# Two fixed places for the experts' weights, filled by indirect gathers on GpSimd that leave out what is already there

## The chip, the core and the metric

The kernel runs on one core of a Trainium2 chip. A core has TensorE (PE, matrix products, with a weight load PEld that runs beside them), VectorE (DVE), ScalarE (ACT), GpSimd (POOL) and SyncE (SP), each with a queue of instructions that it works through in order. DMAs are issued from the queues of SP and POOL here and run on 16 DMA engines. The metric is the device time in microseconds; the kernel before has a median of 381.64 us over 9 runs (379.18 to 387.53 and one of 994.7).

## The reference

2048 rows of 512 features go through a layer norm, and two branches are added to the input: an RWKV attention (three projections, a scan over time, an output projection) and a mixture of 12 experts, of which 8 have weights and 4 pass their input through. Each row goes to its two best experts.

```python
xn = _layernorm(x, axis=-1)
x = x + _L0_attn_ref(xn, ...) + _L0_ffn_ref(xn, ...)

# the expert branch, E = 8 experts with weights, 4 without
probs = softmax(xn @ classifier_w.T)
_, idx = top_k(probs + e_score_correction_bias, 2)
rw = take_along_axis(probs, idx) * 1.5
w_full = sum(one_hot(idx, 12) * rw)
act = silu(xn @ gate_w[e].T) * (xn @ up_w[e].T)      # 512 -> 256, twice
out = sum over e < 8 of w_full[e] * (act @ down_w[e].T)   # 256 -> 512
out = out + xn * sum(w_full[8:])
```

## The kernel before

All products are in float32. The kernel has three parts.

First come the norms (`norm`, L207), the transposes of the normalised rows (`turn_block`, L237), and the router. The normalised rows are also stored to a DRAM tensor `xs` (256 KB per 128 rows), from which the experts' rows are read again. From the router's choice DVE works out a list of tiles: the rows of one expert fill tiles of 128, and the tiles of expert 0 come first, then those of expert 1 and so on. There are 25 tiles in the unrolled code (`TILES`) and a loop for up to 40 (`MAX_TILES`), which this input does not enter. `place_tiles` (L647 to L661) makes `which`, the number of the expert of each tile, and `which_i`, the same as integers; the lines up to L722 make `token_i` (the row that each place of a tile takes), `to_i` (where its result goes) and `wplace` (its weight). These are 128x40 tiles, one column per tile.

Second come the 25 tiles, interleaved with the projections, the scans of the attention and the output projections of the first two blocks of rows. Each tile i is worked in two halves (L847 to L876), five steps of which matter here:

- `gather(i)` (L727): an indirect DMA on POOL reads the tile's 128 rows of 2 KB from `xs` into `xg`, which has two buffers.
- `flip(i)` and `unite(i)` (L769, L777): ACT splits each float into halves of 16 bits (`xp`), a DMA transpose issued from SP turns them (`xq`), and ACT puts them together (`xgT`).
- `fetch(i)` (L738) and `fetch_down(i)` (L751): SP reads the expert's number into a register and issues plain loads of 1 MB (`gw`: gate and up weights) and 0.5 MB (`dw`: down weights), in two alternating buffers each. A load can start when the products of the tile two ahead are done with its buffer.
- `up(i)` (L786) and `activate(i)`: eight instructions of TensorE into `pg`, then tanh on ACT and two products on DVE; `flip_act` and `unite_act` turn the result as above (`ap`, `aq`, `actT`).
- `finish(i)` (L830): four instructions of TensorE into `po`, ACT scales them into `yo`, and an indirect DMA on POOL adds the rows to the output in DRAM. Each such scatter waits for the one before it to land, as both write the output. `add_row` (L963) adds finished rows of the attention to the output, from POOL too.

The order on every queue is written out in the program: `plan` (L988) gives each piece of work a time on a common scale, and the pieces are emitted in order of time. `first_half(i)` emits the products into `pg`, then `fetch(i + 2)` and `gather(i + 3)`; `second_half(i)` emits `flip(i + 2)`, `finish(i - 2)` and `fetch_down(i)`. So the scatter of tile i - 2 stands ahead of the gather of tile i + 4 on POOL, and the loads and the transposes share SP's queue. Before all that, L934 to L953 issue the first two gathers, the loads of the first two tiles, and the first flips; `deferred` (L940) are two DVE adds.

Third, the last blocks of the attention: output rows are read back (`read_out`, L891) when all scatters have landed, the last products are added, and the rows are stored.

Of the kernel before, what the change touches and what calls it, by code (L numbers as in the profile page):

```python
# [59 lines left out]
def layer(ctx: ExitStack, tc: tile.TileContext, x, w_rvk, w_out, decay, first, cls, ebias, gu, down, out):  # L60
# [586 lines left out]
    def place_tiles():  # L647

        later = carve([MAX_TILES, E - 1])
        nc.vector.tensor_tensor(  # L650
            later,
            tiles_f.unsqueeze(2).to_broadcast([P, MAX_TILES, E - 1]),
            ends[:, : E - 1].unsqueeze(1).to_broadcast([P, MAX_TILES, E - 1]),
            ALU.is_ge,
        )
        which = rp.tile([P, MAX_TILES + 1], F32, tag="which", name="which")
        nc.vector.tensor_reduce(which[:, :MAX_TILES], later, AX.X, ALU.add)
        nc.vector.tensor_copy(which[:, MAX_TILES:], ends[:, E - 1 :])
        which_i = const.tile([P, MAX_TILES + 1], I32, tag="which_i", name="which_i")
        nc.vector.tensor_copy(which_i, which)  # L660
        return which_i  # L661


    NK = 2 * NT
# [4 lines left out]
    for m in range(2):  # L669
        ks = slice(m * NT, (m + 1) * NT)  # L670
        nc.vector.tensor_tensor(
            lowhot[:, ks, :],
            lane.unsqueeze(1).to_broadcast([P, NT, P]),
            low[:, m].unsqueeze(2).to_broadcast([P, NT, P]),
            ALU.is_equal,
        )
        nc.vector.tensor_tensor(
            hh,
            tiles128.unsqueeze(1).to_broadcast([P, NT, MAX_TILES]),
            high_b[:, m].unsqueeze(2).to_broadcast([P, NT, MAX_TILES]),  # L680
            ALU.is_equal,
        )
        tok = place.tile([P, NT, NV, MAX_TILES], BF16, tag=f"s{7 + m}", name=f"tok{m}")
        nc.vector.tensor_tensor(  # L684
            tok,
            hh.unsqueeze(2).to_broadcast([P, NT, NV, MAX_TILES]),
            vals[:, m].unsqueeze(3).to_broadcast([P, NT, NV, MAX_TILES]),
            ALU.mult,
        )
        for j in range(NT):  # L690
            k = m * NT + j
            nc.tensor.matmul(pi, lowhot[:, k, :], tok[:, j], start=(k == 0), stop=(k == NK - 1))
        if m == 0:
            which_i = place_tiles()
            fill(5)
    nc.vector.tensor_scalar_mul(wdec, wdec, -1.0)
    cfac = const.tile([P, CC], F32, tag="cfac", name="cfac")
    nc.vector.tensor_add(cfac, first_sb, wdec)
# [36 lines left out]
        )  # L735
        st[i] = {"xg": xg}

    def fetch(i, which=which_i):  # L738

        e = nc.values_load(  # L740
            which[0:1, i : i + 1],
            engines=(SP,),
            min_val=0,
            max_val=E - 1,
            skip_runtime_bounds_check_because="a sum of E - 1 comparisons",
        )
        w = place.tile([P, CC, 2 * INTER], F32, tag=f"s{7 - i % 2}", name=f"gw{i}")
        nc.sync.dma_start(w, gu[bass.ds(e, 1)].rearrange("o p c n -> p (o c) n"))
        st[i].update(w=w, e=e)

    def fetch_down(i):  # L751
# [78 lines left out]
    def finish(i, weight=wplace, to=to_i):  # L830
        po = ps_o.tile([P, C], F32, tag="o", name=f"po{i}")
        for c in range(IC):
            nc.tensor.matmul(  # L833
                po, st[i]["actT"][:, c, :], st[i]["d"][:, c, :], start=(c == 0), stop=(c == IC - 1)
            )
        yo = rows.tile([P, C], F32, tag="rb", name=f"yo{i}")
        nc.scalar.activation(yo, po, AF.Identity, scale=weight[:, i : i + 1])  # L837
        nc.gpsimd.indirect_dma_start(  # L838
            out=out,
            out_offset=bass.IndirectOffsetOnAxis(ap=to[:, i : i + 1], axis=0),  # L840
            in_=yo,
            in_offset=None,
            compute_op=ALU.add,
        )
        del st[i]
# [17 lines left out]
    def second_half(i, n):  # L863

        if i + 1 < n:
            unite(i + 1)
        if i + 2 < n:
            flip(i + 2)
        if i > 1:
            finish(i - 2)  # L870
        if 1 < i < n - 1:
            fetch_down(i)
        if i == n - 2:
            fetch_down(i + 1)
        if i == n - 1:
            finish(i - 1)  # L876
# [156 lines left out]
    with tc.If(count > TILES):  # L1033
        with tc.For_i(TILES, MAX_TILES, 1) as i:
            cols = {}
            for name, a, dt in (
                ("which", which_i, I32), ("token", token_i, I32), ("to", to_i, I32), ("weight", wplace, F32)
            ):
# [4 lines left out]
            fetch_down(0)  # L1043
            turn(0)
            up(0, range(CC))
            activate(0)
# [51 lines left out]
```

## Time and profile before

| | |
|---|---|
| median of 9 runs | 381.64 us |
| profiled execution | 378.44 us, its span 376.7 us |
| TensorE busy | 358.2 us (95% of the span), clock 1.0 |
| DVE busy | 308.7 us (82%) |
| ACT busy | 161.6 us (43%) |
| POOL busy | 91.4 us (24%) |
| bytes moved by DMA | 88.80 MB: 67.85 issued from SP, 20.71 from POOL |
| gw loads | 25 of 1024 KB, 5.6 us from issue to landing (median) |
| dw loads | 25 of 512 KB, 6.9 us |
| gathers of rows (xg) | 25, 5.4 us to landing, 1.15 us of POOL each (mean) |
| scatters to the output | 25, 6.7 us to landing, 1.75 us of POOL each (mean) |
| transposes xq | 25, 6.1 us to landing |

Lines of the profile begin with a time where they come from the timeline: start and length in us, the engine, the line of the kernel (L792), the operation, the tile written and the tiles read, how many instructions were merged (x8), and in brackets how long the engine had been idle and what released it. SPq is SP's queue. In the first view of the page, a row of 40 digits shows the busy share of 40 equal slices of the span, 9 being 90% or more. A line of the waits has the waiting engine and line, whom it waited for, the total in us, how often, and the longest.

### The profile page before, as it was taken

What the parts mean: (1) busy time and instruction counts of PE and PEld (TensorE: products, weight loads), DVE (VectorE), ACT (ScalarE), POOL (GpSimd) and SP (SyncE); (2) the same over time, 40 slices, a digit from 0 to 9 for tenths busy, and PEclk for the clock granted to TensorE, in tenths of its full rate; (3) what the DMA queues carried; (4) which work ended last, traced back from release to release, by engine and by line L of the source; (5) the groups of instructions that cost most, each with busy time, mean ns of one, the idle gap of its engine ahead of it and who ended that gap; (6) DMA issues with size and microseconds to landing.
All of it is one profiled execution on the core that took longest, in us unless ns stands there. A gap on an engine that the chain in (4) does not pass through costs nothing.

```text
span 376.7 us, 3504 instructions
## 1 busy us (share of the span) xinstructions
PE 358.2 (95%) x970; PEld 164.9 (44%) x970; DVE 308.7 (82%) x450; ACT 161.6 (43%) x274; POOL 91.4 (24%) x118
## 2 busy tenths in 40 slices
PE   0999998998999999999999999999999999999995
PEld 0565444443444444444444444444444444444343
DVE  5879899989997997986987769597769786959951
ACT  2777210322554555554556463545254556423000
POOL 5000200220202233322232224143145231122420
PEclk9999999999999999999999999999999999999999
DMA  8997944643667989999799998999999999877494
GB/s 288 404 371 285 335 141 167 224 111 112 181 153 200 258 254 260 215 260 269 217 240 269 266 266 227 262 257 311 259 286 250 302 277 262 157 247 167 87 199 135
DMA packets 63029, 88.80 MB, mean 236 GB/s; under 512 B 42208, under 2 KB 42592, under 8 KB 59232
## 3 DMA queue, kind: packets, MB, share of 16 engines
q1 hardware_dynamic: 55472, 67.85, 61.3%
q0 software_dynamic: 7536, 20.71, 24.1%
q8 instruction: 8, 0.13, 0.1%
q14 instruction: 13, 0.11, 0.1%
HBM read 63.78 MB, written 19.40 MB: 221 GB/s over the span
## 4 chain that ended last, share of the span: by engine, by line
PE 76%; DVE 18%; ACT 3%; issue 2%; DMA 1%; SPq 0%; DVEq 0%; ACTq 0%
PE pg L792 22%; PE po L833 10%; PE pr L408 9%; PE py L325 9%; PE pw L970 7%; PE pz L325 6%; PE px L325 5%; PE pw L918 4%; DVE den L504 3%; DVE tok L684 2%; PE pt L245 1%; DMA x<-in_x_dram 1%; DVE st L212 1%; DVE sums L489 1%; DVE obv L476 1%
## 5 line engine op out<-in xcount | busy, mean ns | idle before, releaser
L792 PE MATMUL pg<-gw,xgT 128*128 128x512 f32 x200 | 90.2, 593 | 1.5 <-ACT xgT L780 1.5
L838 POOL DMA_INDIRECT out_dram<-yo,to_i x25 | 43.8, 1751 | 155.9 <-ACT yo L837 84.6
L408 PE MATMUL pr<-xnT,wrvk 128*128 128x512 f32 x128 | 60.6, 593 | 0.0
L792 PEld LDWEIGHTS pg<-gw,xgT 128*128 128x128 f32 x200 | 37.8, 190 | 49.3 <-issue 45.9
L504 DVE RECIPROCAL den<-den 128x512 f32<-128x512 f32 x16 | 53.5, 3346 | 0.0
L833 PE MATMUL po<-dw,actT 128*128 128x512 f32 x100 | 46.9, 593 | 0.5 <-ACT actT L811 0.5
L800 ACT ACTIVATE th<-pg 128x256 f32<-128x256 f32 x25 | 9.6, 385 | 85.5 <-PE pg L792 85.5
L730 POOL DMA_INDIRECT xg<-xs,token_i x25 | 28.7, 1150 | 61.6 <-ACT xp L772 28.0
L801 DVE SCALAR_TENSOR_TENSOR th<-th,pg 128x256 f32<-128x256 f32 x25 | 10.5, 418 | 32.4 <-ACT th L800 32.2
L408 PEld LDWEIGHTS pr<-xnT,wrvk 128*128 128x128 f32 x128 | 24.1, 190 | 29.2 <-issue 29.2
L325 PE MATMUL px<-xnT,wrvk 128*128 128x512 f32 x64 | 32.3, 604 | 0.0
L780 ACT COPY xgT<-xq 128x1024 uint16<-128x1024 uint16 x25 | 29.0, 1159 | 4.7 <-DMA xq<-xp 4.7
L325 PE MATMUL py<-t,wrvk 128*128 128x512 f32 x64 | 30.7, 594 | 0.0
L918 PE MATMUL pw<-wout_sb,yT 128*128 128x512 f32 (+1 forms) x72 | 28.2, 548 | 2.0 <-DVE xrows L931 1.5
L970 PE MATMUL pw<-wout_sb,yT 128*128 128x512 f32 x64 | 30.1, 592 | 0.0
L833 PEld LDWEIGHTS po<-dw,actT 128*128 128x128 f32 x100 | 18.9, 190 | 24.2 <-issue 22.7
L772 ACT COPY xp<-xg 128x1024 uint16<-128x1024 uint16 x25 | 26.2, 1046 | 5.5 <-DMA xq<-xp 4.3
L837 ACT ACTIVATE yo<-po,wplace 128x512 f32<-128x512 f32 x25 | 17.2, 688 | 22.5 <-PE po L833 22.5
L489 DVE TENSOR_TENSOR_SCAN sums<-obv,state,a 128x512 f32<-128x512 f32 x16 | 20.5, 1282 | 4.0 <-ACT obv L482 3.8
L491 DVE TENSOR_TENSOR_SCAN sums<-obv,state,a 128x512 f32<-128x512 f32 x16 | 20.5, 1284 | 0.6
L918 PEld LDWEIGHTS pw<-wout_sb,yT 128*128 128x128 f32 x72 | 13.5, 190 | 17.0 <-issue 13.4
L476 DVE TENSOR_TENSOR_SCAN obv<-wdec,state,k 128x512 f32<-128x512 f32 x16 | 20.5, 1279 | 0.0
(169 smaller groups left out, 458.1 us busy)
## 6 DMA issues: line engine op xcount, KB each, us to landing
gw<-in_gu_dram SPq DMA_DIRECT2D x25, 1024.0 KB, 5.6
dw<-in_down_dram SPq DMA_DIRECT2D x25, 512.0 KB, 6.9
x<-in_x_dram SPq DMA_DIRECT2D x16, 256.0 KB, 5.4
xs<-x SPq DMA_DIRECT2D x16, 256.0 KB, 7.3
wrvk<-in_w_rvk_dram SPq DMA_DIRECT2D x3, 1024.0 KB
xrow<-xs SPq DMA_DIRECT2D x8, 256.0 KB, 6.1
out_dram<-xrow POOLq DMA_DIRECT2D x8, 256.0 KB, 8.0
xrows<-xs SPq DMA_DIRECT2D x8, 256.0 KB, 5.4
```

The source lines that it names most:

```text
L325: nc.tensor.matmul(ps, a[:, k, c * P : (c + 1) * P], x[:, k], start=(start and k == 0), stop=(k == 1), skip_group_check=True,)
L408: nc.tensor.matmul(ps, wrvk_sb[0][:, k, c * P : (c + 1) * P], xnT[b][:, k, :], start=(k == 0), stop=(k == CC - 1))
L476: nc.vector.tensor_tensor_scan(o2, w.to_broadcast([P, TB]), k, s[:, 0:1], ALU.add, ALU.max)
L504: nc.vector.reciprocal(den, den)
L730: nc.gpsimd.indirect_dma_start(out=xg, out_offset=None, in_=xs, in_offset=bass.IndirectOffsetOnAxis(ap=token[:, i : i + 1], axis=0),)
L772: nc.scalar.copy(xp, st[i]["xg"].bitcast(U16).rearrange("p (c h) -> p h c", h=2))
L780: nc.scalar.copy(xgT.bitcast(U16).rearrange("p c (t h) -> p c t h", h=2), st[i]["xq"].rearrange("p (h c) t -> p c t h", h=2),)
L792: nc.tensor.matmul(pg, st[i]["xgT"][:, c, :], st[i]["w"][:, c, :], start=(c == 0), stop=(c == CC - 1))
L833: nc.tensor.matmul(po, st[i]["actT"][:, c, :], st[i]["d"][:, c, :], start=(c == 0), stop=(c == IC - 1))
L838: nc.gpsimd.indirect_dma_start(out=out, out_offset=bass.IndirectOffsetOnAxis(ap=to[:, i : i + 1], axis=0), in_=yo, in_offset=None, compute ...
L918: nc.tensor.matmul(po[:, hs], yT[b][:, c, j * P : (j + 1) * P], wout_sb[:, c, hs], start=(c == 0), stop=(c == CC - 1),)
L970: nc.tensor.matmul(po, yT[b][:, c, j * P : (j + 1) * P], wout_sb[:, c, :], start=(c == 0), stop=(c == CC - 1))
```

## The change

The places for the weights are no longer taken anew for every tile. Two places for `gw` and two for `dw` are made once, and tile i uses place i % 2 of each. They are filled by indirect gathers issued from POOL: partition p of a place takes row 128 e + p of the weights, seen as 1024 rows of 8 KB (gate and up) or 4 KB (down). The rows' numbers come from `place_rows`, five DVE instructions on 128x40 or 128x38 elements that stand after the last router products are issued: `all_i` holds the number 128 e + p for each tile, and `new_i` the same plus 8192 where the tile two ahead has the same expert. A number beyond the last row is out of bounds, and such rows are not copied. The last tile's down weights go to a place of their own and take `all_i`.

The loads leave SP's queue, and SP reads no expert's number any more. `fetch(i + 2)` stays in `first_half(i)`, so it is now on POOL ahead of `gather(i + 3)`. `fetch_down(i)` moves from the end of `second_half(i)` into `finish(i - 2)`, after its products and ahead of its scatter on POOL. The first two tiles' loads stand on POOL behind the first two gathers. The loop for further tiles uses `all_i`.

```diff
+    def place_rows():
+        row = rp.tile([P, MAX_TILES], F32, tag="row", name="row")
+        nc.vector.tensor_scalar(row, which[:, :MAX_TILES], float(P), tok_p, ALU.mult, ALU.add)
+        all_i = const.tile([P, MAX_TILES], I32, tag="all_i", name="all_i")
+        nc.vector.tensor_copy(all_i, row)
+        same = rp.tile([P, MAX_TILES - 2], F32, tag="same", name="same")
+        nc.vector.tensor_tensor(same, which[:, 2:MAX_TILES], which[:, : MAX_TILES - 2], ALU.is_equal)
+        nc.vector.scalar_tensor_tensor(row[:, 2:], same, FAR, row[:, 2:], ALU.mult, ALU.add)
+        new_i = const.tile([P, MAX_TILES], I32, tag="new_i", name="new_i")
+        nc.vector.tensor_copy(new_i, row)
+        return all_i, new_i
...
         if m == 0:
-            which_i = place_tiles()
+            which, which_i = place_tiles()
             fill(5)
+    all_i, new_i = place_rows()
     nc.vector.tensor_scalar_mul(wdec, wdec, -1.0)
...
-    def fetch(i, which=which_i):
-        e = nc.values_load(
...
-        w = place.tile([P, CC, 2 * INTER], F32, tag=f"s{7 - i % 2}", name=f"gw{i}")
-        nc.sync.dma_start(w, gu[bass.ds(e, 1)].rearrange("o p c n -> p (o c) n"))
...
+    gws = [place.tile([P, CC, 2 * INTER], F32, tag=f"s{7 - n}", name=f"gw{n}") for n in range(2)]
+    dws = [dwp.tile([P, IC, C], F32, tag="dw", name=f"dw{n}") for n in range(2)]
+
+    def load_rows(t, a, rows_i, i):
+        nc.gpsimd.indirect_dma_start(
+            out=t.rearrange("p c n -> p (c n)"),
+            out_offset=None,
+            in_=a.rearrange("e p c n -> (e p) (c n)"),
+            in_offset=bass.IndirectOffsetOnAxis(ap=rows_i[:, i : i + 1], axis=0),
+            bounds_check=E * P - 1,
+            oob_is_err=False,
+        )
+
+    def fetch(i, rows_i=new_i):
+        load_rows(gws[i % 2], gu, rows_i, i)
+        st[i]["w"] = gws[i % 2]
+
+    def fetch_down(i, rows_i=new_i):
+        d = dws[i % 2]
         if i == TILES - 1:
-            d = place.tile([P, IC, C], F32, tag=f"s{6 + i % 2}", name=f"dw{i}")
-        else:
-            d = dwp.tile([P, IC, C], F32, tag="dw", name=f"dw{i}")
-        nc.sync.dma_start(d, down[bass.ds(st[i]["e"], 1)].rearrange("o p c n -> p (o c) n"))
+            d, rows_i = place.tile([P, IC, C], F32, tag=f"s{6 + i % 2}", name=f"dw{i}"), all_i
+        load_rows(d, down, rows_i, i)
         st[i]["d"] = d
...
             nc.tensor.matmul(
                 po, st[i]["actT"][:, c, :], st[i]["d"][:, c, :], start=(c == 0), stop=(c == IC - 1)
             )
+        if 1 < i + 2 < TILES - 1 and weight is wplace:
+            fetch_down(i + 2)
         yo = rows.tile([P, C], F32, tag="rb", name=f"yo{i}")
...
         if i > 1:
             finish(i - 2)
-        if 1 < i < n - 1:
-            fetch_down(i)
         if i == n - 2:
             fetch_down(i + 1)
```

More of the change, by code (lines that the diff above doesn't have):

```diff
@@ L660, in place_tiles @@
         nc.vector.tensor_copy(which_i, which)
-        return which_i
+        return which, which_i
+    def place_rows():
[9 more added lines that the diff above has]
+        return all_i, new_i
     NK = 2 * NT
@@ L736, in gather @@
         st[i] = {"xg": xg}
-    def fetch(i, which=which_i):
-        e = nc.values_load(
[L741 to L745, printed above, removed]
-        )
-        w = place.tile([P, CC, 2 * INTER], F32, tag=f"s{7 - i % 2}", name=f"gw{i}")
-        nc.sync.dma_start(w, gu[bass.ds(e, 1)].rearrange("o p c n -> p (o c) n"))
-        st[i].update(w=w, e=e)
-    def fetch_down(i):
+    gws = [place.tile([P, CC, 2 * INTER], F32, tag=f"s{7 - n}", name=f"gw{n}") for n in range(2)]
[8 more added lines that the diff above has]
+            oob_is_err=False,
+        )
+    def fetch(i, rows_i=new_i):
[3 more added lines that the diff above has]
+        d = dws[i % 2]
         if i == TILES - 1:
-            d = place.tile([P, IC, C], F32, tag=f"s{6 + i % 2}", name=f"dw{i}")
-        else:
-            d = dwp.tile([P, IC, C], F32, tag="dw", name=f"dw{i}")
-        nc.sync.dma_start(d, down[bass.ds(st[i]["e"], 1)].rearrange("o p c n -> p (o c) n"))
+            d, rows_i = place.tile([P, IC, C], F32, tag=f"s{6 + i % 2}", name=f"dw{i}"), all_i
+        load_rows(d, down, rows_i, i)
         st[i]["d"] = d
@@ L1036, in layer @@
             for name, a, dt in (
-                ("which", which_i, I32), ("token", token_i, I32), ("to", to_i, I32), ("weight", wplace, F32)
+                ("which", all_i, I32), ("token", token_i, I32), ("to", to_i, I32), ("weight", wplace, F32)
             ):
@@ L1042, in layer @@
             fetch(0, cols["which"])
-            fetch_down(0)
+            fetch_down(0, cols["which"])
             turn(0)
```

## The prediction

> **What bounds the kernel now.** The page's first two parts come first. The span is 376.7 us (378.44 with what lies around it; the nine runs shown have a median of 381.64, 3.2 above this profiled one).
>
> ```profile
> span 376.7 us, 3504 instructions
> PE 358.2 (95%) x970; PEld 164.9 (44%) x970; DVE 308.7 (82%) x450; ACT 161.6 (43%) x274; POOL 91.4 (24%) x118
> PE   0999998998999999999999999999999999999995
> DMA  8997944643667989999799998999999999877494
> PE 76%; DVE 18%; ACT 3%; issue 2%; DMA 1%; SPq 0%; DVEq 0%; ACTq 0%
> ```
>
> TensorE is busy in every slice but the first and last. The last line is the chain that ended last: three quarters TensorE, and no load of an expert's weights on it. The windows view of the tiles' stage (busy us and instruction count of each engine, then clock, DMA share, GB/s), and all waits of TensorE:
>
> ```profile
> 94.00:333.00 239.00, 238.71 (x557) 105.65 (x558) 196.87 (x242) 120.64 (x202) 67.99 (x49) 1.00 0.96 248
> ```
>
> ```profile
> PE pt L245 <- DVE x L232: 9.5, 1, 9.5
> PE pg L792 <- ACT xgT L780: 1.5, 1, 1.5
> PE pw L918 <- DVE xrows L931: 1.5, 1, 1.5
> PE pi L692 <- DVE tok L684: 1.4, 1, 1.4
> PE po L833 <- ACT actT L811: 0.5, 1, 0.5
> PE pw L918 <- DVE orows L927: 0.5, 1, 0.5
> ```
>
> From 94 to 333 us TensorE works 238.71 of 239.00 us at full clock, though the DMA engines are nearly always busy (0.96). No wait names gw or dw. So bytes saved there buy nothing on TensorE: what can move are the stretch before 94 us, a cover in the middle that is lost, and the tail. The issue table and the POOL timeline give the prices:
>
> ```profile
> gw<-in_gu_dram SPq DMA_DIRECT2D x25, 1024.0 KB, 5.6
> dw<-in_down_dram SPq DMA_DIRECT2D x25, 512.0 KB, 6.9
> xg<-xs,token_i POOLq DMA_INDIRECT x25, 5.4
> xq<-xp SPq DMA_TRANSPOSE x25, 6.1
> ```
>
> ```profile
> 306.84 1.66 POOL L838 DMA_INDIRECT out_dram<-yo,to_i  x1 [7.88 <-ACT yo L837]
> 308.80 1.17 POOL L730 DMA_INDIRECT xg<-xs,token_i  x1 [0.30 <-issue]
> ```
>
> In the first four lines the last number is the median time in us from issue to landing; in the two of the timeline an indirect DMA holds POOL 1.17 to 1.66 us, the next one follows after 0.30, and a wait in front holds back all that is queued behind it.
>
> **What is saved.** The reference's router with its seed-0 inputs puts 593, 657, 231, 136, 364, 238, 373, 199 rows on the eight experts: 5, 6, 2, 2, 3, 2, 3, 2 tiles of 128, which is exactly 25. An expert's tiles from its third on copy nothing: tiles 2, 3, 4, 7, 8, 9, 10, 17, 22. Sixteen tiles still load. 9 x 1.5 MB (1.573e6 bytes) is 14.2 of 88.8 MB. The saving is mostly early; from tile 11 on only two of 14 tiles skip.
>
> **Five small DVE instructions (place_rows).** The nearest rows are the 128x40 ones at L711 to L721, which start 0.10 to 0.27 us apart (67.70, 67.93, 68.03, 68.30, 68.42): 5 x 0.21 = 1.05 us, between 0.9 and 1.2. They stand where DVE has no gap from 51 to 72 us, ahead of the tokens, so token_i comes at 69.2 instead of 68.1, and both deferred adds (L941) move by as much. TensorE next needs DVE at py: the third product of the py group at 70.25 starts at 73.69 (two of 1.72 us before it) and needs the L368 add, done at 73.3. That becomes 74.4, so TensorE loses 0.75 us. DVE's idle 0.57 + 1.01 + 0.19 us before 82.5, where it waits for TensorE, absorbs the rest. The chain from there to the second pg (94.27) has no slack: den, reciprocal, obv, the exponential, the xgT copy, all back to back. **+0.75 us.**
>
> **The first four loads move from SP to POOL.** On SP they go out at 59.8, 60.4, 67.0 and 67.5. On POOL they stand behind gather(0) and gather(1), which wait for token_i: gathers at 69.4 and 70.8, loads at about 72.1, 73.5, 74.9, 76.3 (1.15 + 0.30 each), gather(2) at 77.7 instead of 75.4. gw of tile 0 lands 5.6 to 6.7 us after issue, about 79; pg(0) starts at 83.98, so this lateness is hidden, and gather(2) is wanted at 94.12. But 3 MB now run while the first transposes run. ACT stood still there already:
>
> ```profile
> 74.11 1.05 ACT L772 COPY xp<-xg 128x1024 uint16<-128x1024 uint16 x1 [0.72 <-DMA xg<-xs,token_i]
> 79.50 1.05 ACT L772 COPY xp<-xg 128x1024 uint16<-128x1024 uint16 x1 [4.34 <-DMA xq<-xp]
> 80.45 1.16 ACT L780 COPY xgT<-xq 128x1024 uint16<-128x1024 uint16 x1
> ```
>
> xp of tile 1 waits for the transpose of tile 0 (issued 75.18, landed 79.5: 4.3 us) and blocks ACT, with the first xgT behind it. In the new kernel xp(0) follows the exponentials, which move with DVE: 74.45, so the transpose goes out at 75.6. If it lands at L, pg(0) can start at L + 2.2 (copies of 1.05 and 1.16). TensorE's 1.55 us gap before pg(1) and the 0.75 absorb lateness until pg(0) at 86.3, thus L of 84.1. As in the old run (4.3) L is 79.9; at the longest xq landing in the trace (9.6) it is 85.2, 1.1 past the point. I take the 9.6, since more load bytes are in flight here than beside any xq of the trace: **+1.0 us**; bounds 0 and, starved until all loads are through, the second rival's price. Here a rule bears. The Trainium skill, DMA: Bandwidth & Descriptors, under Issuing engines are not separate DMA queues, says that DMAs of sync and gpsimd run on the same 16 engines and interleave, so that spreading them saves only issue time; it speaks against any gain by the second queue. By its figure for a 1 MB gpsimd load (6.15 us, section Bandwidth) gw would land about half a us later than the 5.6, still hidden.
>
> **The loads in the body: 0.** Per tile of 10.3 us POOL has a scatter and a gather, 1.75 + 1.15 + 0.6. Two more indirect DMAs of 1.15 + 0.30 make 6.4 us: no bound. Their price is bounded by 0.95 (shortest gather) and 2.49 (longest scatter); at 2.49 each the tile needs 9.1, still under 10.3. I take the gather's 1.15, as it is the same kind with the same 128 rows, only 8 or 4 KB instead of 2. What matters is the order. fetch(i+2) waits on POOL for pg(i), and gather(i+3) queues behind it; in the old order it followed the scatter. For tile 6 the gather moves from 114.5 to 118.7, and xp wants it at 130.4: 11.7 us left for a landing of 5.4 to 7.4 plus perhaps 5 behind the megabyte on the same queue. For tiles 13 to 16 some 10.8 to 12 us are left, also enough. SP loses its waits for PE (4.7 + 5.6 + 1.9) and transposes leave no later. fetch_down stands before the scatter of the same tile and delays it by 0.5 us; nobody waits for scatters there. The tightest tiles are 23 and 24. Row adds issued at 297.07 hold the scatter of tile 18 until 306.84; now fetch(23) goes out behind it at about 308.8 (SP: 304.83) and must land by 318.7, 9.9 us against 4.7 to 6.7. gather(24) goes at 310.2 (before: 308.80), wanted by ACT at 316.0. ACT would stand perhaps 2 us, but TensorE wants its xgT only at 328.99, which needs the gather by 319.1.
>
> **The tail: 0**, between -1 and +1. After 333 DVE's scans and the last products lead; the scatter chain (332.66, 338.28, 343.87, 349.58, each behind the last one's landing) has 2.7 us to spare, DVE's idle before L927 at 369.11. dw of tile 24 goes out after the scatter of tile 21, at some 331 to 334 instead of 327.1, and po(24) wants it at 341.3.
>
> **Sum.** 378.44 + 0.75 + 1.0 = 380.2 for a run like the profiled one; set on the median, 381.64 + 1.75 = 383.4. Own range of this case: +0.75 to +3.
>
> **Rivals.** *A lost cover in the body (slower).* The one place is gather(24) behind fetch(23) behind the held scatter. It decides when xg lands over 8.9 us after issue (310.2 to 319.1). For it: the trace's landings of 4.2 to 7.4 are without a megabyte ahead in the same queue; with 5.6 more, 13 us, xp ends at 324.3, the transpose (7.6 there) at 332, xgT at 333 to 334.5, and TensorE stands 4 to 5.5 us at pg(24). Against: the bytes ahead, some 1.8 MB at 272 GB/s (the windows view from 225 to 300 us), are through in 6.7 us. With the forecast's 1.75 it gives 387 to 389.
>
> *Starved transposes at the start (slower).* Should the packets of xq run only after the 3 MB, from 73.5 at 404 GB/s (the best slice) or 248 (the body's rate), they end at 81.3 or 86.2; plus 4.3, pg(0) starts at 87.8 or 92.7 and pg(1) is 2.1 or 7.0 us late: 383.7 to 388.6. The same skill page, Queues, rings and completion order, has each engine alternate between queues by packets, not bytes. With 8 KB rows on one side that would favour the loads; no run here shows it yet.
>
> *Relief (faster).* With 14 MB gone the first scatters and transposes land sooner, and ACT's 4.34 us standstill and the 1.55 us gap could go; the gap is all that TensorE can win before 333, the tail perhaps 1 more: -2.5, 379.1. Against: that gap hangs on DVE's chain, not a DMA, and the first two tiles load in full.
>
> *The skip does not skip.* If a row out of bounds costs its transfer or its slot time, traffic stays at 88.8 MB: 382 to 386, as forecast with tighter slack.
>
> **Chances.** Forecast 0.50 (within 0.5% in 0.35 of it, 0.15 slower); lost cover 0.20, slower; starved start 0.12, slower; relief 0.10 (0.08 faster, 0.02 same); no skip 0.08 (0.03 same, 0.05 slower). 0.5%, 1.9 us, is about what a measurement of this kernel can tell from no change. Together: faster 0.08, same 0.40, slower 0.52. The range reaches from most of the relief, 379.6, to the starved start's far end, 388.6.
>
> **What would show it.** Traffic near 74.6 MB; 50 POOL gathers of about 1.15 us at the new load lines; five DVE rows of 0.2 us ahead of the wdec one; pg(1) at 95 to 97; TensorE without a wait from there to 333. A TensorE wait for gw, dw or xgT in that stretch makes this wrong, as does a POOL gather of 3 us or more.

## The result, and the profile after

The changed kernel takes a median of 399.19 us over 10 runs (388.02 to 423.83), the kernel before 381.84 us over 31 runs. The ratio is **1.027, 95% interval 1.021 to 1.033**: slower by some 10 us. (The ratios here compare the executions within 1.5% of the fastest of their kernel, for this one 4 of 12, so its longer times, up to 423.83, are not in them; where a version has too few for a ratio, the median of all is given.) The profiled execution took 392.09 us, 13.65 above the profiled one of before. Its page:

```profile
span 390.3 us, 3443 instructions
PE 363.0 (93%) x970; PEld 165.7 (42%) x970; DVE 310.3 (80%) x455; ACT 161.8 (41%) x274; POOL 148.8 (38%) x168
PE   0999998969999999999999999799999999799985
DMA  8996910672355786765879999899979999977393
DMA packets 63028, 74.65 MB, mean 191 GB/s; under 512 B 44512, under 2 KB 44896, under 8 KB 60384
PE 54%; DMA 18%; DVE 18%; ACT 6%; issue 3%; SPq 0%; DVEq 0%; POOL 0%; POOLq 0%; ACTq 0%
```

The saving took place: 74.65 MB instead of 88.80. But the row of TensorE now has weak slices (the 9th, 26th and 35th of 40), and DMA's part of the chain that ended last went from 1% to 18%. Of TensorE's waits one line has grown (1.5 us before) and one is new:

```profile
PE pg L812 <- ACT xgT L800: 8.2, 4, 3.9
PE po L853 <- ACT actT L844: 2.1, 1, 2.1
```

xgT and actT are what ACT makes of a landed transpose, so the next view is the waits of ACT, of after and then of before (total, times, longest, in us):

```profile
ACT ap L837 <- DMA aq<-ap: 22.6, 9, 4.2
ACT xgT L800 <- DMA xq<-xp: 19.7, 7, 7.2
ACT xp L792 <- DMA xq<-xp: 11.4, 1, 11.4
```

```profile
ACT xgT L780 <- DMA xq<-xp: 4.7, 4, 1.8
ACT xp L772 <- DMA xq<-xp: 4.3, 1, 4.3
ACT ap L817 <- DMA aq<-ap: 0.3, 1, 0.3
```

No row of TensorE names gw or dw: the loads are in time. What comes late is the transposes, 9 us of such waits having become 54. Their times from issue to landing, shortest, median and longest: xq 3.1, 6.1 and 15.7 us (before 3.1, 6.1 and 9.6), aq 2.4, 4.0 and 8.7 (before 3.0, 3.8 and 5.4). These are the landings that the profile could match, 15 of 25 xq and 6 of 23 aq (before 7 and 4); the chain that ended last holds one more aq, of 12.3 us, issued at 322.38. The median of xq hasn't moved; the long ones have.

The windows view (busy us and count of PE, PEld, DVE, ACT, POOL; then clock, DMA share, GB/s) shows where that matters:

```profile
94.00:150.00 56.00, 56.00 (x132) 24.88 (x131) 50.95 (x63) 28.05 (x48) 26.00 (x20) 1.00 0.61 129
150.00:225.00 75.00, 75.00 (x176) 33.18 (x175) 59.88 (x75) 39.24 (x69) 38.58 (x30) 1.00 0.78 169
225.00:300.00 75.00, 71.50 (x167) 31.03 (x166) 57.50 (x69) 35.88 (x59) 36.11 (x31) 1.00 1.03 221
300.00:333.00 33.00, 32.18 (x76) 14.11 (x75) 25.18 (x30) 15.13 (x25) 16.92 (x13) 1.00 1.04 202
```

To 225 us, where most skips lie, the DMA engines have room (0.61 and 0.78; before 0.80 and 0.97) and TensorE loses nothing. Nearly every tile loads again from 182 us on, and the row adds (`add_row`) start at 237. From 200 to 225 us, with loads and no row add yet, the share is 0.95 and TensorE still loses nothing (25.00 of 25.00 us). From 225 to 300 the share is 1.03, as full as before (1.05), but 221 GB/s get through instead of 272 (fewer bytes are wanted, too: 243 suffice in experiment 2 below), and TensorE stands.

**The first loss, 4.4 us before 99 us.** Timeline:

```profile
75.89 0.99 POOL L758 DMA_INDIRECT dw<-in_down_dram,new_i  x1 [0.30 <-issue]
...
86.38 1.04 ACT L792 COPY xp<-xg 128x1024 uint16<-128x1024 uint16 x1 [11.36 <-DMA xq<-xp]
87.33 1.15 ACT L800 COPY xgT<-xq 128x1024 uint16<-128x1024 uint16 x1
...
88.53 5.18 PE L812 MATMUL pg<-gw,xgT 128*128 128x512 f32 x8 [3.89 <-ACT xgT L800]
...
98.70 1.88 PE L812 MATMUL pg<-gw,xgT 128*128 128x512 f32 x4
```

The last of the first four loads goes out at 75.89. The first transpose, issued at 75.05, lands at 86.3 after 11.2 us; the second, alone at 87.45, takes 3.1. TensorE stands 3.89 us at pg(0), and the eight products then take 5.18 us instead of 3.60, because the granted clock is 0.54 from 88 to 90 us and 0.61 from 90 to 92. pg(1) starts at 98.70 instead of 94.27. While the first transpose runs, from 78 to 82 us, the two queues have (packets, MB, share of 16 engines):

```profile
q0 software_dynamic: 272, 1.51, 97.2%
q1 hardware_dynamic: 143, 0.04, 4.7%
```

Each issuing engine has such a queue of DMAs of its own, called its ring here. q0 is POOL's ring with the loads, q1 SP's with the transpose. The transpose gets a third of the packets and 5% of the engines' time, and its packets are small (some 0.3 KB on average), the loads' of 8 or 4 KB.

**The second loss, from tile 16 on.** The lag is how much later a product starts than in the old kernel. From tile 6 to 15 it is a constant 4.0 us. Then:

```profile
239.41 1.61 POOL L758 DMA_INDIRECT dw<-in_down_dram,new_i  x1 [0.30 <-issue]
...
252.60 1.16 ACT L800 COPY xgT<-xq 128x1024 uint16<-128x1024 uint16 x1 [7.19 <-DMA xq<-xp]
...
253.81 3.70 PE L812 MATMUL pg<-gw,xgT 128*128 128x512 f32 x8 [3.01 <-ACT xgT L800]
...
336.31 2.83 PE L853 MATMUL po<-dw,actT 128*128 128x512 f32 x4 [2.07 <-ACT actT L844]
```

The transpose of tile 16 is issued at 236.83 and lands at 252.5, 15.7 us later; in the old kernel it took 9.6, and pg(16) started at 246.59, now 253.81. So the lag is 7.2 there, 8.2 at pg(19) (285.68 against 277.49), 9.3 at pg(21), 11.6 at po(21) and 13.4 at pg(24), which is the whole loss at the end. (A listed gap is a few tenths smaller than what the schedule loses there, as the ends of matmuls are modelled: 0.49 listed before pg(19), 0.9 lost.) At pg(21) a gather took part: it stood on POOL behind a scatter that had waited 7.20 us for row adds, xp waited 1.63 us for it at 295.27, and the transpose behind it then took 9.7. Two loads are in flight with the transpose of tile 16, gw issued at 233.90 and dw at 239.41, and two row adds at 237.17. From 240 to 244 us the queues show

```profile
q1 hardware_dynamic: 622, 0.38, 49.1%
q0 software_dynamic: 212, 0.49, 61.1%
```

and in the old kernel, where the same two loads stood on SP's ring ahead of and behind the transpose, from 239 to 243 us, just before it landed:

```profile
q1 hardware_dynamic: 1182, 0.61, 68.5%
q0 software_dynamic: 205, 0.35, 48.0%
```

About twice as many packets of SP's ring get through there in the same four microseconds (in after 512 more from 244 to 248 us and 703 from 248 to 252). In the four microseconds before these windows it is the other way round: SP's ring gets 190 packets through in the old kernel, where the transpose stands behind the megabyte, and 423 in after. So here, on one ring, the transpose waits for the load ahead of it and then goes quickly; on two rings it starts at once and is drawn out.

### The profile page after: what moved, and what is told of

It reads as the page before. It is cut to its first block, busy times and chain, and to the rows that moved or that the text cites. A ratio compares the mean times of both kernels' runs of the same rounds, so it can differ in the third digit from the quotient of the medians.

```text
span 390.3 us, 3443 instructions
## 1 busy us (share of the span) xinstructions
PE 363.0 (93%) x970; PEld 165.7 (42%) x970; DVE 310.3 (80%) x455; ACT 161.8 (41%) x274; POOL 148.8 (38%) x168
## 2 busy tenths in 40 slices
DMA packets 63028, 74.65 MB, mean 191 GB/s; under 512 B 44512, under 2 KB 44896, under 8 KB 60384
## 4 chain that ended last, share of the span: by engine, by line
PE 54%; DMA 18%; DVE 18%; ACT 6%; issue 3%; SPq 0%; DVEq 0%; POOL 0%; POOLq 0%; ACTq 0%
PE pg L812 17%; PE po L853 7%; PE pr L408 6%; PE py L325 5%; DMA xq<-xp 5%; DMA out_dram<-yo,to_i 5%; PE pz L325 5%; PE px L325 4%; PE pw L939 4%; DMA aq<-ap 3%; PE pw L991 3%; DVE den L504 3%; DMA out_dram<-xrow 2%; DVE tok L698 2%; DMA xg<-xs,token_i 2%
## 5 line engine op out<-in xcount | busy, mean ns | idle before, releaser
L812 PE MATMUL pg<-gw,xgT 128*128 128x512 f32 x200 | 92.0, 602 | 8.2 <-ACT xgT L800 8.2
L861 POOL DMA_INDIRECT out_dram<-yo,to_i x25 | 42.6, 1705 | 56.9 <-DMA out_dram<-xrow 18.1
L853 PE MATMUL po<-dw,actT 128*128 128x512 f32 x100 | 48.0, 604 | 2.6 <-ACT actT L844 2.1
L758 POOL DMA_INDIRECT gw<-in_gu_dram,new_i x25 | 27.7, 1109 | 57.5 <-PE pg L812 54.8
L758 POOL DMA_INDIRECT dw<-in_down_dram,new_i x24 | 29.3, 1220 | 29.4 <-PE po L853 26.0
L800 ACT COPY xgT<-xq 128x1024 uint16<-128x1024 uint16 x25 | 28.9, 1157 | 19.7 <-DMA xq<-xp 19.7
L837 ACT COPY ap<-act 128x512 uint16<-128x512 uint16 x23 | 14.1, 614 | 25.4 <-DMA aq<-ap 22.6
L489 DVE TENSOR_TENSOR_SCAN sums<-obv,state,a 128x512 f32<-128x512 f32 x16 | 20.6, 1284 | 4.1 <-ACT obv L482 2.5
```

The costliest lines, as they stand in the source:

```text
L758: nc.gpsimd.indirect_dma_start(out=t.rearrange("p c n -> p (c n)"), out_offset=None, in_=a.rearrange("e p c n -> (e p) (c n)"), in_offset= ...
L800: nc.scalar.copy(xgT.bitcast(U16).rearrange("p c (t h) -> p c t h", h=2), st[i]["xq"].rearrange("p (h c) t -> p c t h", h=2),)
L812: nc.tensor.matmul(pg, st[i]["xgT"][:, c, :], st[i]["w"][:, c, :], start=(c == 0), stop=(c == CC - 1))
L853: nc.tensor.matmul(po, st[i]["actT"][:, c, :], st[i]["d"][:, c, :], start=(c == 0), stop=(c == IC - 1))
L861: nc.gpsimd.indirect_dma_start(out=out, out_offset=bass.IndirectOffsetOnAxis(ap=to[:, i : i + 1], axis=0), in_=yo, in_offset=None, compute ...
```

## The experiments

The theories in the expectations: *S*, transposes come late beside loads that run on another ring than theirs; *Q*, it is the order of the work in POOL's queue; *I*, the indirect load is slow by itself. A later rival of S is the time at which the loads are issued. The experiments are named by the first part of their labels (e1, e2).

**1. The first four loads back on SP** (`e1_head_sp`), all else as after.

```diff
     for i in range(2):
-        fetch(i)
-        fetch_down(i)
+        e = nc.values_load(
+            which_i[0:1, i : i + 1],
...
+        )
+        nc.sync.dma_start(gws[i], gu[bass.ds(e, 1)].rearrange("o p c n -> p (o c) n"))
+        nc.sync.dma_start(dws[i], down[bass.ds(e, 1)].rearrange("o p c n -> p (o c) n"))
+        st[i].update(w=gws[i], d=dws[i])
```

> The changed kernel, but the first two tiles' loads are plain loads from SP again, where they stood before. Theory S (transposes starve beside loads on another ring): the first xq lands in about 4.3 us instead of 11.2, TensorE's gap of 3.9 us at 88.5 and the slowed products behind it go, pg of tile 1 starts near 95 (94.3 plus the 0.4 to 0.75 of place_rows): 4 us less than the changed kernel, the later stalls stay, ratio to the kernel before about 1.015 to 1.02. Theory Q (POOL's order holds the gathers back): the start gains the same, as gather(2) moves up as well, but nothing else changes. Theory I (an indirect load is slow by itself): no gain over 1 us at the start, as only four of 50 loads are changed.

Median 397.12 us (388.14 to 410.33). The start is mended: pg(0) at 84.99 and

```profile
95.28 3.70 PE L812 MATMUL pg<-gw,xgT 128*128 128x512 f32 x8 [1.55 <-ACT xgT L800]
```

with the old gap of 1.55 us and 1.0 us later than before (of it 0.3 by a later start of the whole router; the rest, 0.7, is place_rows). But the profiled execution lost 7.59 us at one later pg and 13 in all, so the 4 us expected do not show in the total, which is about that of after. The four loads on POOL are the cause of the first loss, and the second is independent of it and varies from run to run. This trace has every landing, and around the 7.59 us everything in flight is late, not the transposes alone: issued between 281 and 291 us, gw takes up to 16.4 us, dw 15.9, xg 15.5, xq 16.5 and aq 19.7 (longest in e2 below: 6.8, 10.9, 11.0, 9.4 and 5.3). No row add is in flight then; one pair had landed by 278.6, the next goes out at 310.5.

**2. The saving alone, loads on SP** (`e2_skip_sp`): the kernel before with the two fixed places, its plain loads left on SP and nine pairs left out by a list.

```diff
+WHICH = [e for e, n in enumerate((5, 6, 2, 2, 3, 2, 3, 2)) for _ in range(n)]
...
     def fetch(i, which=which_i):
+        st[i].update(w=gws[i % 2], has=has(i, which))
+        if st[i]["has"]:
+            return
```

> The kernel before with fixed places, loads from SP as before, and the nine loads that repeat an expert left out by a list that is fixed for this input (no place_rows, no load on POOL). It moves the same bytes as the changed kernel. If saved bytes buy time: 2 us or more less than before. By the forecast's reading (no load on the chain): within 1.5 us of before, and TensorE without a wait from 94 to 333 us. If the two fixed places cost something by their own waits: slower by 1 us or more.

380.03 us, ratio **1.000 (0.996 to 1.004)**, with 74.64 MB. xq lands in 3.0 to 9.4 us, and the window from 225 to 300 us is full:

```profile
225.00:300.00 75.00, 75.00 (x176) 33.23 (x175) 61.06 (x77) 36.69 (x60) 26.05 (x20) 1.00 1.00 243
```

The same bytes are saved, and nothing is won and nothing lost. So saved bytes buy nothing on SP's ring, and the loss comes with the move.

**3. Plain loads from POOL** (`e5_pool_plain`): after, with the indirect loads replaced by plain ones at the same places of POOL's queue; a skipped one issues nothing.

```diff
     def load_rows(t, a, rows_i, i):
+        if rows_i is new_i or (rows_i is all_i and i == TILES - 1):
+            if i < 2 or WHICH[i] != WHICH[i - 2]:
+                nc.gpsimd.dma_start(t, a[WHICH[i]])
+            return
```

> The changed kernel with its loads on POOL as plain DMAs of a fixed expert (list for this input), at the same places; a skipped load issues nothing at all. Theory I: the loss against the kernel before shrinks to under 1%, since no row list, no bounds and no empty DMA is left. Theories S and Q: nearly the whole loss stays (1.02 to 1.03), the first xq lands in 10 us or more, and xq in the crowded stretch behind the row adds in 12 us or more; by Q some 2 us come back, since nine loads that wait for pg in front of a gather are gone, by S none.

Median 397.63 us (384.69 to 405.33), as after, though one of the four times is within 1% of before. xq takes up to 23.4 us, aq up to 20.6, and one gap of TensorE is

```profile
303.60 6.06 PE L817 MATMUL pg<-gw,xgT 128*128 128x512 f32 x8 [14.26 <-ACT xgT L805]
```

POOL is busy only 110.4 us instead of 148.8. Theory I falls with this trace, and with experiment 6, which has a ratio: neither the indirect form, nor its list of rows, nor POOL's time in it is needed for late transposes.

**4. No skipping** (`e3_no_skip`): after with `all_i` everywhere.

```diff
-    def fetch(i, rows_i=new_i):
+    def fetch(i, rows_i=all_i):
...
-    def fetch_down(i, rows_i=new_i):
+    def fetch_down(i, rows_i=all_i):
```

> The changed kernel with every load copied in full (all_i for all tiles), so 14 MB more on POOL's ring. Theory S: the stretch from 100 to 215 us, quiet in the changed kernel, now has late xq (8 us or more in the median instead of 6.1) and TensorE stalls there too: 5 to 20 us slower than the changed kernel. Theory Q: the same waits as in the changed kernel, since a skipped load holds POOL as long as a full one: within 3 us of it. Theory I as Q.

Median 433.05 us (415.92 to 437.04) with 88.80 MB; TensorE waits 49.9 us for xgT in five gaps, xq takes up to 25.9 us. So the skip works and is worth some 34 us in this layout (28 between the fastest of each), while on SP's ring the same bytes cost nothing. But the standstills that were expected from 100 to 215 us did not come: TensorE works 75.00 of 75.00 us from 150 to 225, with every load on POOL's ring and a DMA share of 0.95. Behind the one at the start, its four gaps all lie after 270 us.

**5. The order on POOL** (`e4_order`): the gather ahead of the fetch, the scatter ahead of the fetch_down.

```diff
-        if i + 2 < n:
-            fetch(i + 2)
...
             gather(i + 3)
+        if i + 2 < n:
+            fetch(i + 2)
```

> The changed kernel with two swaps on POOL: the gather of rows ahead of fetch in each tile, and the scatter ahead of fetch_down. Theory Q (POOL's order does it: gathers and scatters wait behind the loads): most of the loss after 225 us goes, 5 us or more less than the changed kernel, ACT's waits for xg and POOL's for the row adds shrink. Theory S (transposes lose against loads on another ring): the same loads still run beside the same transposes, xq lands in up to 12 us or more, the time stays within 4 us of the changed kernel (median 399).

Median 412.2 us (401.25 to 425.0): worse by 13, not better. ACT's waits for the transposes are still there, larger for aq (41.8 us in all, after: 22.6). The gain that theory Q expected isn't there; that the time stays within 4 us of after, as expected under S, isn't so either. Why this order is worse wasn't followed further.

**6. The loads on ACT's ring** (`e11_act_ring`): as after, but the body's loads by a list from ACT's queue, the first four from SP, none on POOL.

```diff
-                nc.gpsimd.dma_start(t, a[WHICH[i]])
+                nc.scalar.dma_start(t, a[WHICH[i]])
```

> Same bytes as the changed kernel and no load on POOL: plain loads by a list fixed for this input, issued from ACT's queue right behind the tanh and the scaling that have waited for the same products anyway; the first four from SP. So the loads have a ring of their own beside the transposes', but neither POOL's order nor its descriptors. Theory S: transposes starve as in the changed kernel, xq up to 12 us or more, TensorE waits for xgT after 225 us, 1.01 to 1.04 of before. Theory Q: within 1% of the kernel before, as POOL is as free as it was there. A third one (only rings that POOL fills do it): also within 1%, xq at most 10 us.

397.58 us, ratio **1.041 (1.034 to 1.049)**. POOL's work is that of before (91.8 us), and the transposes are late all the same. The longest standstill of ACT, with what the queues did from 212 to 216 us while that transpose (issued 203.69) was under way:

```profile
222.38 1.16 ACT L805 COPY xgT<-xq 128x1024 uint16<-128x1024 uint16 x1 [11.03 <-DMA xq<-xp]
...
223.59 6.26 PE L817 MATMUL pg<-gw,xgT 128*128 128x512 f32 x8 [6.90 <-ACT xgT L805]
```

```profile
q10 hardware_dynamic: 48, 0.22, 73.2%
q0 software_dynamic: 42, 0.09, 55.2%
q1 hardware_dynamic: 147, 0.03, 6.1%
```

q10 is ACT's ring. 48 packets of a load held the engines for 73% of those 4 us, 147 of the transpose for 6%. S stands: no load is in POOL's queue, and the loss is there. Nor had any row add been issued by then:

```profile
L990 POOL DMA_DIRECT2D out_dram<-xrow x8: 888/966/1298, 241.7 to 381.6; - x8
```

(shortest, median and longest time in ns, then the first and the last start in us).

**7. No row adds** (`e10_no_row_adds`): six of the eight left out, all but the last two, of the third part.

```diff
             for n in (i - 1, i) if j % 2 else ():
-                add_row(n)
+                pass
```

> The changed kernel without the adds of finished attention rows from POOL between the tiles (the output lacks the attention of six groups of 128 rows of its first half). Theory Q: the scatters no longer wait up to 10.9 us for row adds, nor the loads behind them; the stalls at 246 to 256 and 280 to 290 us go and only the start's 4.4 us stays: 383 to 387 us. Theory S: 3 MB less traffic, some relief, but late transposes stay wherever a load runs: 388 to 396.

385.02 us, ratio **1.012 (1.006 to 1.019)**. The start loses as in after, and in the body nearly nothing (75.00 of 75.00 us from 225 to 300, one gap of 0.36 behind). This is the time that was expected under Q (383 to 387 us), not under S (388 to 396). It is e11, with the loads off POOL's queue, that speaks against Q. With the loads on POOL, the row adds bring nearly all of the second loss; but they need not be in flight when transposes are late, as the longest gaps of e1 and e11 show.

**8. Only the start, on ACT's ring** (`e7_act_head`): the kernel before, with its first four loads issued from ACT behind the first flip.

```diff
-        fetch(i)
-        fetch_down(i)
...
     flip(0)
+    for i in range(2):
+        nc.scalar.dma_start(gw0[i], gu[0])
+        nc.scalar.dma_start(dw0[i], down[0])
```

> The kernel before, where only the first four loads move: plain, of expert 0, from ACT's queue between the first two flips, so that they run beside the first transpose as in the changed kernel, but from ACT's ring and not POOL's. Theory S: the first xq lands in 9 us or more instead of 4.3, TensorE's gap before the first two pg grows and pg of tile 1 starts at 97 to 100 us instead of 94.3: 3 to 5 us slower than before. If only rings filled by POOL do it: xq within 6 us, and less than 1.5 us slower.

381.1 us, ratio 1.002 (0.997 to 1.007). The mechanism is there, but the 3 to 5 us expected of it are not:

```profile
84.89 1.04 ACT L772 COPY xp<-xg 128x1024 uint16<-128x1024 uint16 x1 [10.17 <-DMA xq<-xp]
...
87.05 3.70 PE L792 MATMUL pg<-gw,xgT 128*128 128x512 f32 x8 [2.50 <-ACT xgT L780]
```

The first transpose takes 10.1 us (74.74 to 84.85) where before it took 4.3. From 78 to 82 us the loads' ring has 233 packets and 1.41 MB, the transpose's 102 and 0.03. The gap is 2.50 us instead of after's 3.89, without place_rows' 0.75 us and with the last load out at 74.74 instead of 75.89; the clock doesn't drop, and pg(1) is 1.5 us late instead of 4.4. In after, 1.4 us more of gap brought the clock's 1.6 with it.

**9. Rows of 2 KB** (`e13_small_rows`): experiment 6 with each load as two DMAs, so that a row is 2 KB.

```diff
-                nc.scalar.dma_start(t, a[WHICH[i]])
+                for h in range(2):
+                    if t.shape[1] == CC:
+                        nc.scalar.dma_start(t[:, h::2, :], a[WHICH[i]][:, h::2, :])
...
```

> The kernel with loads from ACT's ring (1.041 of before), each load now two DMAs that take every second 2 KB piece (gw) or one half of the row (dw), so its rows are 2 KB and not 8 and 4. Same bytes, same places, same time of issue. Theory S as turns by packets (each engine serves the rings in turn, a 256 byte packet of a transpose against a whole row): with rows a quarter as long the transposes get through sooner, xq and aq land in at most 10 us, and the loss shrinks to 1.00 to 1.02. If it is the time of issue or the third ring alone: 1.03 to 1.05 as before. If short rows cost throughput: worse, 1.05 or more.

389.59 us, ratio **1.017 (1.008 to 1.027)**: better than with large rows (1.041). xq still takes up to 16.9 us.

**10. Both causes taken away** (`e14_head_no_adds`): experiments 1 and 7 together; against e1:

```diff
             for n in (i - 1, i) if j % 2 else ():
-                add_row(n)
+                pass
```

> The changed kernel with the first four loads from SP and without the row adds between the tiles (the output lacks the attention of six groups of 128 rows), so both places of the loss are gone. If the account is complete: 0.7 us (place_rows) over the kernel before, ratio 0.998 to 1.006, TensorE without a wait from 96 to 333 us. If POOL's loads cost something else in the body as well: 1.01 or more.

381.44 us, ratio **0.999 (0.994 to 1.004)**. With the first four loads on SP and no row adds, everything else of the change, the loads on POOL, the skips, place_rows and the orders, costs no more than the interval leaves room for (some 0.4%). So the two losses make up the whole, as far as the ratio goes. But the expected body without a wait isn't there: without a row add xq still takes up to 14.5 us and aq up to 13.1, TensorE stands once in the body,

```profile
318.23 1.98 PE L853 MATMUL po<-dw,actT 128*128 128x512 f32 x4 [2.85 <-ACT actT L844]
```

and one of the ten times is 397.27 us, where before has none above 388 but its 994.7.

**11. The start with rows of 2 KB** (`e7b_head_small_rows`): experiment 8, each load as two DMAs; against e7:

```diff
-        nc.scalar.dma_start(gw0[i], gu[0])
-        nc.scalar.dma_start(dw0[i], down[0])
+        for h in range(2):
+            nc.scalar.dma_start(gw0[i][:, h::2, :], gu[0][:, h::2, :])
+        for h in range(2):
+            nc.scalar.dma_start(dw0[i][:, h : h + 1, :], down[0][:, h : h + 1, :])
```

> The first four loads from ACT's queue beside the first transpose (where its xq took 10.1 us), now in 2 KB rows. By turns of packets: 1056 packets of the transpose against 1536 of the loads instead of 384, so the transpose is through after about two thirds of the loads: xq in 7 to 8.5 us. If the loads go first whatever their rows: 10 us again.

A miss: the first transpose takes 14.1 us instead of 10.1, TensorE stands 6.56 us, one time of 386.42. From 82 to 86 us the two rings get equal numbers of packets (from 78 to 82 it is 480 to 314),

```profile
q10 hardware_dynamic: 419, 0.82, 74.5%
q1 hardware_dynamic: 422, 0.11, 13.5%
```

so the small rows do bring the turns nearer to even. But the loads became slower (from 78 to 82 us 263 GB/s in all instead of 424) and so lasted longer beside the transpose.

**12 and 13. The time of issue.** In `e18_sp_early`, experiment 2 with the gw load 2 to 3 us sooner, ahead of aq on SP's ring; in `e19_act_late`, experiment 6 with it 2 to 3 us later, behind the next flip. The time differs between POOL, ACT and SP, and could have been the cause in place of the ring.

The edit of e18, against e2:

```diff
             fetch(i + 2)
+        if 0 < i < n - 1:
+            send_act(i - 1)
```

The edit of e19, against e11:

```diff
-        if i + 2 < n:
-            fetch(i + 2)
...
             flip(i + 2)
+            fetch(i + 2)
```

> Loads from SP with the nine left out by the list (ratio 1.000 so far), but each gw stands on SP ahead of the tile's aq transpose, so it is issued 2 to 3 us sooner, right when pg is done, as on the rings of POOL and ACT. Ring and order of issue are told apart: if loads and transposes on one ring is what keeps the kernel whole, still 0.997 to 1.008, with aq up to 8 us behind the megabyte. If the early start of gw is what makes transposes late: TensorE waits for xgT or actT after 225 us, 1.015 to 1.04.

> The kernel with loads from ACT's ring (1.041), each gw issued 2 to 3 us later, behind the copy for the next xq, when the tile's aq has had its time: the time of issue that it has on SP. If an own ring beside the transposes is the cause: still 1.02 to 1.045, xq or aq over 12 us. If the time of issue is: 1.00 to 1.01.

e18: 380.09 us, ratio **0.998 (0.990 to 1.007)**. e19: 393.15 us, ratio **1.030 (1.019 to 1.041)**. Windows from 225 to 300 us, e18 and then e19:

```profile
225.00:300.00 75.00, 75.00 (x176) 33.16 (x175) 61.13 (x76) 37.86 (x60) 24.40 (x20) 1.00 1.05 235
```

```profile
225.00:300.00 75.00, 70.36 (x160) 30.54 (x159) 55.68 (x68) 32.39 (x53) 20.92 (x16) 0.98 1.02 217
```

Sooner on SP's ring costs TensorE nothing, although ACT waits 21.6 us for aq there (a wait of ACT alone, with slack behind it); later on ACT's ring it still loses 4.6 us in this window. The ring decides.

**What stands.** Loads on a ring of their own, POOL's or ACT's, beside the transposes on SP's make the transposes land late in places where the DMA engines are full; ACT works in order and stands, and TensorE behind it. On SP's ring, in the order of issue with the transposes, the same loads do no harm. e2 against e11 shows it, and e5 in its trace; e18 and e19 hold it against the time of issue. With the loads on POOL's ring the row adds are part of it: e10 and e14 lose little in the body without them. A full share alone is not enough (e3 from 150 to 225 us).

The Trainium skill, DMA: Bandwidth & Descriptors, section Issuing engines are not separate DMA queues, states that DMAs of different issuing engines run on the same 16 engines and interleave, and that spreading them saves only issue time. The runs agree that it wins nothing (e11 against e2); they add that it can cost 4%. The same page, Queues, rings and completion order, has each engine take turns between rings by packets. The counts of 419 to 422 with 2 KB rows look like such turns, and so does the time share of 97% to 5% with large rows. But the counts of 480 to 314, 272 to 143 and 233 to 102 are not one to one. The page's packet is a bundle of several descriptors, and no run shows how the packets that the profile counts relate to it.

**What stays open.** What happens in the engines. At the start the loads run well (386 GB/s over all queues from 78 to 82 us in after) and the transpose waits beside them; in the body's standstills the loads and gathers are as late as the transposes (e1), and the engines are held without moving much: in e11 a load's packet held an engine for 1.0 us (48 packets, 73% of 16 engines for 4 us), at the start of after for 0.23. So "the loads are favoured" describes the start, not the body. Smaller rows helped in the body and hurt at the start. Why a full share of the engines moves less when the rings mix (217 GB/s in e19 at 1.02, 235 in e18 at 1.05; 184 in e1 from 284 to 300 us) wasn't found. Nor how the row adds take part: they run in POOL's ring in every version, and cost nothing beside loads on SP's ring. They hold POOL's queue (10.88 us until 251.90), and what is queued behind them then goes out close together, eight DMAs from 279.45 to 290.44 us in e1; whether this bunching does it, no run tells. Nor was the transpose tried on the loads' ring, which would tell "one ring" from "SP's ring".

No version beat both kernels: e2 and e18 are level with before.

## Why the prediction was wrong

It said 383.4 us, 379.6 to 388.6; by the ratio the kernel takes some 392. The direction was the likelier one given (0.52).

- **What bounds the kernel** was read rightly: no load on the chain, bytes saved buy nothing (e2: 1.000).
- **place_rows, +0.75 us: right.** Five DVE rows from 65.07 to 65.89, and 0.7 us at pg(1) in e1.
- **The first four loads, +1.0 us: the mechanism right, the size wrong.** Gathers predicted at 69.4 and 70.8 came at 69.1 and 70.5, loads predicted from 72.1 to 76.3 at 71.7 to 75.9. The longest landing in the trace, 9.6 us, was taken for the first transpose, and it took 11.2: by the formula of that step L - 84.1 = 2.2 instead of 1.0. The other 1.6 us wasn't in the sum at all: the clock fell after a 3.89 us gap. 0.75 + 2.2 + 1.6 = 4.55, measured 4.4. This is the rival of the starved transposes, to which 0.12 was given, within its 2.1 to 7.0 (2.2 to 7.1 by the step's own formula), though part of the transpose did run beside the loads (143 packets from 78 to 82 us).
- **The loads in the body, 0: this step failed.** What it counted was right: the indirect loads held POOL 1.11 and 1.22 us each (1.15 taken), POOL was no bound, and no load set TensorE back (a gather had a share in the 1.0 us at pg(21)). It failed in the half sentence that transposes "leave no later". They do leave in time; they *land* later. Each queue was followed to the moment of issue, and the landing was taken over from a trace in which loads and transposes shared one ring. The trace of before had no row for a transpose beside a load on another ring in this stage, and the step should have bounded that, as the step on the start did; the 2.1 to 7.0 of that rival, paid a second time where the DMA share is 1.05, would have been the bound. Measured: 9.4 us from tile 16 on (13.4 - 4.0), and next to nothing there in e10, without the row adds; the step did not ask what these bring beside the loads.
- **Rival "a lost cover in the body"**: a cover was lost, but not at gather(24) (ACT stood 3.98 us for its rows at 328.92, and pg(24) had no gap), and mainly by transposes, from tile 16; e11 loses without any load in POOL's queue.
- **Rival "relief"**: no, e2 has the saving without any gain. **Rival "the skip does not skip"**: no, 74.65 MB against 74.6 predicted, and e3 shows what it would have been.
- **The tail, 0: right.** The lag at pg(24) is 13.4 us and at the end 13.6.
- **The range** left out that two of its cases can come together: the starved start and a loss in the body.

## What to carry to other kernels

When a transfer moves to another issuing engine, ask not only when it leaves but what it then runs beside: in one ring it took its place in order of issue here, in a second ring it shared the engines with what the compute waits for. In this kernel it paid to keep the bulk loads on the ring of the short, urgent transposes, ordered by need. A reading such as "DMA share 0.96, TensorE 100%" doesn't tell how much slack the landings have, and saved bytes elsewhere need not give them any: try the move with the DMAs that it will run beside.

## What the runs showed of the hardware that was not expected

- **The clock of TensorE falls after a gap.** Eight products took 3.60 to 3.70 us after gaps of 2.50 (e7), 2.81 (e3), 2.87 (e1) and 3.01 us (after), but 5.18 after 3.89 (after), 5.40 after 4.00 (e19), 6.26 after 6.90 (e11) and 6.06 after 14.26 (e5). So these gaps of 3.89 us and more cost some 1.5 to 2.6 us on top of themselves. It isn't quite a rule: in after, four products took 2.83 instead of 1.88 behind a gap of 2.07 us at 336, with the clock at 0.50 from 338 to 340 us, and in e1 eight took 5.14 behind one of 2.52 at 325. The Trainium skill, TensorE: Matmul & The Clock Gate, Part 1, states half clock after an idle window of about 3.4 us that runs freely; the longer gaps agree, those of 2.07 and 2.52 us do not.
- **A skipped indirect load costs POOL its full slot**: the gw load of the skipped tiles 2 to 4 and 7 to 10 took 0.99 to 1.04 us of POOL each, that of the loaded tiles 5 and 11 to 15 1.02 to 1.04. Nor do the rows' sizes show there: on average 1.109 us for 128 rows of 8 KB, 1.220 for 4 KB, 1.164 for 2 KB.
- **The spread.** before lies within some 3% (but for one run of 994.7 us), after between 388 and 424: where a transpose lands beyond its slack differs from execution to execution (after and e1 have their gaps at different tiles), and each gap sets all behind it back.
